# A two-layer gated attention and mixture-of-experts kernel: loads and constants enter the written order, layer 2 reuses layer 1's row tables, 256 words between scatters

## The chip, the cores and the metric

The kernel runs on one core of a Trainium2 chip. A core has TensorE (PE, with its weight loads shown apart as PEld), VectorE (DVE), ScalarE (ACT), GpSimd (POOL) and SyncE (SP), each working through its own instructions strictly in the order in which the program lists them. DMA transfers are issued by SP, by ACT and, for the indirect ones, by POOL. The metric is device time in microseconds of one execution; the figure for the kernel before is the median of three runs.

## The reference, cut to what matters

There are 4 sequences of 512 tokens with 128 channels, a context of 77 tokens for each, and two layers. Each layer adds a gated cross-attention (16 heads of 8 channels) and a gated mixture of 8 experts (128 to 512 to 128, the best two experts of each token):

```python
for l in range(2):
    # attention: LayerNorm is taken ahead of it; layer 1 adds position slopes and a mask
    q, k, v = norm(x) @ Wq.T, ctx @ Wk.T, ctx @ Wv.T
    x = x + tanh(g_xattn[l]) * (softmax(q k.T / sqrt(8)) v @ Wo.T + bo)
    # experts
    xf = norm(x)
    probs = softmax(xf @ w_router)
    w, i = top_k(probs, 2)
    x = x + tanh(g_ffn[l]) * sum_k w[k] * (gelu(xf @ w1[i[k]] + b1) @ w2[i[k]] + b2)
```

(The bias `bo` belongs to layer 0 alone.)

## The kernel before

Everything is float32 apart from the layer-1 masks. Four sequences ("batches", n = 0 to 3) go through attention one after another; batches 0 and 1 form routing group 0, batches 2 and 3 group 1. A group's 2048 token-expert pairs are sorted by expert with indirect DMAs: each token row of 130 words (128 channels, the gate weight, and the place its result goes to) is scattered twice into a table in DRAM, `xg`, in which each expert owns a region of 2048 rows. Then 16 blocks per group, 7 of 256 rows and 9 of 128, each load the weights of one expert and a piece of its rows, compute, and scatter their result rows into another table, `yk`, from which each batch loads them again in token order and adds them to x. Rows of `xg` that no token reaches must still be harmless, so the tables are cleared with zeros from a tile `fill` at the start (`clear`, lines 741 to 753), one table per layer and group: four tables, 16 stores of 1040 KB and 4 of 130 KB in all.

Every scatter goes through `Scatters.send` (line 392): POOL first writes 512 zeros into one partition of `fill` (line 394), then issues the indirect DMA (line 395). There are 64 scatters into `xg` and 92 into `yk`, 156 in all.

The order of all work is written out by hand in the string `ORDER` (lines 832 to 875). A word names a part: layer, letter, and after the dot the batch or group. The loop under it emits the instructions of each word on whatever engines it needs, so the string fixes the order on all five engines at once. The words that the text uses:

- `LS` LayerNorm statistics (DVE, then `rstd` on POOL), `LT` normalise (ACT), `LU` transpose (PE, copy on ACT), `Q` queries (PE, ACT)
- `S0` to `S3` scores of 128 tokens (PE) and their maxima (four reductions on DVE); `M`, `W0`, `W1` put the maxima into the queries; `X0` to `X3` scores again, and exp on ACT; `U0` to `U3` sums over the context; `E`, `T`, `N`, `F` the rest of attention
- `RS`, `RT`, `RU`, `RL`, `RC`, `RD`, `RM`, `RN`, `RX` the routing of one batch, up to the row numbers; `Z0` to `Z3` its scatters into `xg`, two for each word
- `RB` the group's table of blocks (DVE), `RG` its transfer into SP's registers (a PE transpose, a DVE copy, then SP reads 16 registers)
- `w`, `x`, `t`, `u`, `d`, `y` with a block number: weight load, row load (both on SP, both needing the registers), transpose, first and second matrix (PE, with GELU on ACT, bias and gate on DVE), scatter into `yk`
- `CL`, `CA` load and add the results of a batch
- `vclear`, `fill`, `clear`, `mask`, `keys`, `values`, `gate`, `routing`, `second` are words without a dot: constants and shared operands

Outside this order stand, before it, all loads of inputs (lines 68 to 98), the constants of the head slots (lines 116 to 144), the ones under the eight exp tiles `eT` (lines 146 to 150) and the zeros of the two `m_pad` tiles (lines 151 to 155). All are emitted ahead of the first word.

Of the kernel before, what the change touches and what calls it, by code (L numbers as in the profile page):

```python
# [8 lines left out]
F32 = mybir.dt.float32  # L9
# [29 lines left out]
SPARE = NFULL * 256 + NTAIL * P  # L39


@with_exitstack
def flamingo_kernel(ctx: ExitStack, tc: tile.TileContext, a: dict, out: bass.AP):
# [24 lines left out]
    x_sb = [wpool.tile([P, NT, D], F32, tag=f"x{b}", name=f"x{b}") for b in range(B)]  # L68

    def load_x(b):  # L70
        nc.sync.dma_start(out=x_sb[b], in_=a["x"][b].rearrange("(p t) d -> p t d", p=P))

    load_x(0)
    ctxT = load("ctxT", [P, B * KV], a["ctxT"], eng=nc.scalar)
    W = [{}, {}]
    for l in range(2):
        W[l]["wk"] = load(f"wk{l}", [P, 2, D], a[f"wk{l}"], eng=nc.scalar)
        W[l]["wq"] = load(f"wq{l}", [P, 2, D], a[f"wq{l}"], eng=nc.scalar)
        if l == 0:
            wv = load("wv", [P, 2 * D], a["wv"], eng=nc.scalar)  # L80
            gates = wpool.tile([P, 4], F32, tag="gates", name="gates")
            nc.scalar.dma_start(out=gates[:, 0:2], in_=a["g_xattn"].partition_broadcast(P))
            nc.scalar.dma_start(out=gates[:, 2:4], in_=a["g_ffn"].partition_broadcast(P))
        W[l]["wo"] = load(f"wo{l}", [D, D], a[f"wo{l}"])
        W[l]["router"] = load(f"router{l}", [D, E], a[f"router{l}"])
        if l == 0:
            load_x(1)
            bo = wpool.tile([P, D], F32, tag="bo", name="bo")
            nc.sync.dma_start(out=bo, in_=a["bo"].partition_broadcast(P))
    load_x(2)  # L90
    load_x(3)
    qpos_i = load("qpos_i", [P, B * NT], a["qpos"], dtype=I32)
    kpos_i = wpool.tile([P, B * KV], I32, tag="kpos_i", name="kpos_i")
    nc.sync.dma_start(out=kpos_i, in_=a["kpos"].partition_broadcast(P))
    msk_i, mskT_i = [], []
    for b in range(B):
        msk_i.append(load(f"msk{b}", [P, NT, KV], a["mask"][b].rearrange("(p t) k -> p t k", p=P), dtype=I32))
        mskT_i.append(load(f"mskT{b}", [KV, S], a["maskT"][b], dtype=I32))
# [3 lines left out]
    make_identity(nc, ident)  # L102
    mhalf = const.tile([P, NT], F32, tag="mhalf", name="mhalf")
# [12 lines left out]
    prow = counted("prow", [P, 1], [[0, 1]], channel_multiplier=1, dtype=I32)  # L116
    slot_i = const.tile([P, 2], I32, tag="slot_i", name="slot_i")
    nc.vector.tensor_scalar(slot_i[:, 0:1], prow, 15, None, ALU.bitwise_and)
    nc.vector.tensor_scalar(slot_i[:, 1:2], prow, 4, 1, ALU.arith_shift_right, ALU.bitwise_and)
    slot = const.tile([P, 2], F32, tag="slot", name="slot")  # L120
    nc.vector.tensor_copy(slot, slot_i)
    row_r = const.tile([P, 1], F32, tag="row_r", name="row_r")
    row_p = const.tile([P, 1], F32, tag="row_p", name="row_p")
    nc.vector.tensor_scalar(row_r, slot[:, 0:1], float(HD), None, ALU.is_equal)
    nc.vector.tensor_scalar(row_p, slot[:, 0:1], float(HD + 1), None, ALU.is_equal)
    base_slope = const.tile([P, 1], F32, tag="base_slope", name="base_slope")
    for g in range(HB):
        nc.vector.memset(base_slope[32 * g : 32 * g + 32, :], SLOPES[4 * g])
    k_scale, k_ones, k_slope = [], [], []
    for w in range(2):  # L130
        own = const.tile([P, 1], F32, tag=f"own{w}", name=f"own{w}")
        nc.vector.tensor_scalar(own, slot[:, 1:2], float(w), None, ALU.is_equal)
        t = const.tile([P, 1], F32, tag=f"k_scale{w}", name=f"k_scale{w}")
        nc.vector.tensor_scalar(t, own, INV_SQRT_HD, None, ALU.mult)
        k_scale.append(t)
        t = const.tile([P, 1], F32, tag=f"k_ones{w}", name=f"k_ones{w}")
        nc.vector.tensor_tensor(t, own, row_r, ALU.mult)
        k_ones.append(t)
        t = const.tile([P, 2], F32, tag=f"k_slope{w}", name=f"k_slope{w}")
        nc.vector.tensor_tensor(own, own, row_p, ALU.mult)  # L140
        nc.vector.tensor_tensor(own, own, base_slope, ALU.mult)
        for h in range(2):
            nc.vector.tensor_scalar(t[:, h : h + 1], own, SLOPES[2 * h + w] / SLOPES[0], None, ALU.mult)
        k_slope.append(t)

    eTs = []
    for i in range(8):
        t = const.tile([P, S], F32, tag=f"eT{i}", name=f"eT{i}")
        nc.vector.memset(t[64:, :], 1.0)
        eTs.append(t)  # L150
    m_pads = []
    for i in range(2):
        t = const.tile([P, NT, 2, P], F32, tag=f"m_pad{i}", name=f"m_pad{i}")
        nc.vector.memset(t, 0.0)
        m_pads.append(t)
# [230 lines left out]
    class Scatters:  # L386
# [5 lines left out]
        def send(self, to, rows, index):  # L392

            nc.gpsimd.memset(fill[:1, 0, :S], 0.0)  # L394
            i = nc.gpsimd.indirect_dma_start(  # L395
                out=to[:, :], out_offset=bass.IndirectOffsetOnAxis(ap=index, axis=0), in_=rows, in_offset=None
            )
            for other in self.sent:
                tc.declare_no_dep(i.ins, other.ins, reason="each pair has a row of its own")
            self.sent.append(i)  # L400


    class Routing:
# [13 lines left out]
        def turn(self):  # L417
# [4 lines left out]
            nc.gpsimd.tensor_copy(self.rows[:, :, :, D + 1], pair_at[:, self.b % 2])  # L422
# [92 lines left out]
        def scatter(self, b, t):  # L515
            rows, to = self.left[b]
            for k in range(2):
                self.scatters.send(xgs[self.l][self.group], rows[:, k, t, :], to[:, k, t : t + 1])
# [58 lines left out]
    class Blocks:  # L577
# [24 lines left out]
        def load_x(self, i):  # L602
            if i >= NBLK:
# [5 lines left out]
                in_=xgs[self.l][self.group][bass.ds(self.r.begins[i], n * P), :].rearrange("(s p) d -> p s d", p=P),  # L609
# [34 lines left out]
        def down(self, i):  # L644
# [23 lines left out]
            nc.vector.tensor_tensor(to[:, :n], x[:, :n, D + 1], spare[:, self.at(i) // P : self.at(i) // P + n], ALU.max)  # L668
# [7 lines left out]
    class Combine:  # L676
# [5 lines left out]
        def load(self):  # L682
            b = self.b
            self.y = act.tile([P, 2, NT, D], F32, tag="y", name="y")
            for k in range(2):
                at = SPARE + k * CAP + b % 2 * S
# [21 lines left out]
    def routing_constants():  # L708
# [4 lines left out]
        for e in range(E):  # L713
# [14 lines left out]
        pair_at = counted(  # L728
            "pair_at", [P, 2, 2, NT], [[S, 2], [CAP, 2], [1, NT]], base=SPARE, channel_multiplier=NT
        )  # L730
        spare = counted("spare", [P, SPARE // P], [[P, SPARE // P]], channel_multiplier=1)
# [3 lines left out]
    fill = const.tile([P, 2, CAP // P * PAY], F32, tag="fill", name="fill")  # L735
    xgs, yks = [], []
    for l in range(2):
        xgs.append([dram.tile([E * REGION, PAY], F32, tag=f"xg{l}{g}", name=f"xg{l}{g}") for g in range(2)])
        yks.append([dram.tile([SPARE + 2 * CAP, D], F32, tag=f"yk{l}{g}", name=f"yk{l}{g}") for g in range(2)])

    def clear(l, g):
        xg = xgs[l][g]
        for e in range(0, E, 2):
# [4 lines left out]
                in_=fill,  # L748
            )
        nc.sync.dma_start(  # L750
            out=xg[UNUSED : UNUSED + 256, :].rearrange("(p r) d -> p (r d)", p=P),
            in_=fill.rearrange("p r f -> p (r f)")[:, : 2 * PAY],
        )
# [39 lines left out]
    msk, mskT = [], []  # L793

    def mask(b):
# [5 lines left out]
        msk.append(m)  # L801
        mskT.append(mT)
# [8 lines left out]
    def part(l, name, n):  # L811
# [21 lines left out]
        vclear3 vclear0 fill vclear2 0LS.0 keys0 gate values0 0LT.0 0LS.2 0LU.0 0LS.1 0LS.3 0Q.0 0LT.1 0LT.2 values3  # L833
        0S1.0 0S0.0 0S2.0 0LU.1 0LU.2 0S3.0 0Q.1 clear10 0M.0 vclear1 mask0 0W0.0 0LT.3 0S0.1 0W1.0 0S3.1 clear00
        0X0.0 0S1.1 0Q.2 values1 mask1 0S2.2 mask2 0X1.0 0S2.1 0U0.0 0M.1 0X2.0 routing 0U1.0 0X3.0 0E0.0 0W0.1 0U2.0
        0X0.1 0T0.0 0U3.0 0X1.1 0W1.1 0U0.1 0E1.0 0S1.2 0U1.1 0T1.0 clear01 mask3 0S0.2 0E0.1 0LU.3 clear11 0N.0 0T0.1
        0X2.1 0F.0 0RS.0 0X3.1 values2 0U2.1 0RT.0 0S3.2 0U3.1 0M.2 0E1.1 second 0Q.3 0W0.2 0RU.0 0T1.1 0W1.2 0S2.3
        0N.1 0RL.0 0RC.0 0F.1 0RS.1 0X0.2 0X1.2 0RD.0 0U0.2 0X2.2 0RM.0 0RN.0 0RX.0 0U1.2 0Z0.0 0RT.1 0S1.3 0U2.2
        0RU.1 0Z1.0 0S3.3 0RL.1 0S0.3 0X3.2 0RC.1 0M.3 0RD.1 0Z2.0 0U3.2 0W0.3 0RM.1 0E0.2 0T0.2 0X0.3 0RN.1 0RX.1
        0RB.1 0E1.2 0Z3.0 0X1.3 0Z0.1 0T1.2 0N.2 0RG.1 0U0.3 0W1.3 0w0.0 0Z1.1 0F.2 0Z2.1 0Z3.1 0x0.0 0U1.3 0RS.2  # L840
        0E0.3 0X2.3 0x1.0 0X3.3 0RT.2 0w1.0 0U2.3 0U3.3 0E1.3 0T0.3 0RU.2 0T1.3 0RL.2 0N.3 0RC.2 0t0.0 0x2.0 0t1.0
        0F.3 0RD.2 0x3.0 0w2.0 0x4.0 0u0.0 0u1.0 0RS.3 0RM.2 0d0.0 0x5.0 0w3.0 0w4.0 0w5.0 0y0.0 0RT.3 0d1.0 0t2.0
        0t3.0 0RN.2 0x6.0 0u2.0 0RU.3 0RX.2 0t4.0 0w6.0 0u3.0 0x7.0 0Z0.2 0d2.0 0u4.0 0t5.0 0RL.3 0t6.0 0d3.0 0x8.0
# [109 lines left out]
```

## Time and profile before

| what | value |
|---|---|
| median of three runs | 453.98 us (452.78 to 454.99) |
| the profiled execution | 449.32 us, its span 447.6 us |
| PE busy | 394.7 us (88%) |
| POOL busy | 296.0 us (66%) |
| DVE busy | 243.9 us (54%) |
| ACT busy | 225.0 us (50%) |
| mean granted TensorE clock | 0.969 |
| moved by DMA | 81.19 MB |

The span runs from the first to the last instruction; the execution's own time lies 1.7 us above it. A busy share is an average over stages with different limits. Matmuls are pipelined and their ends are modelled, so PE counted as busy need not be at full pace. In "out<-in" the names are the program's; "idle before" is the time in which an engine sat before a group's instructions, with what ended most of it.

### The profile page before, as it was taken

What the parts mean: (1) busy time and instruction counts of PE and PEld (TensorE: products, weight loads), DVE (VectorE), ACT (ScalarE), POOL (GpSimd) and SP (SyncE); (2) the same over time, 40 slices, a digit from 0 to 9 for tenths busy, and PEclk for the clock granted to TensorE, in tenths of its full rate; (3) what the DMA queues carried; (4) which work ended last, traced back from release to release, by engine and by line L of the source; (5) the groups of instructions that cost most, each with busy time, mean ns of one, the idle gap of its engine ahead of it and who ended that gap; (6) DMA issues with size and microseconds to landing.
All of it is one profiled execution on the core that took longest, in us unless ns stands there. A gap on an engine that the chain in (4) does not pass through costs nothing.

```text
span 447.6 us, 9040 instructions
## 1 busy us (share of the span) xinstructions
PE 394.7 (88%) x2936; PEld 279.9 (63%) x2936; DVE 243.9 (54%) x929; ACT 225.0 (50%) x529; POOL 296.0 (66%) x480
## 2 busy tenths in 40 slices
PE   2399999979999599999999999999889989998960
PEld 1166345534988489996774355544378878987960
DVE  7777478763746443437682367776256533332442
ACT  3256756646564345356437764544538434433540
POOL 3478312787298889867885430698159988888870
PEclk9999999999999989999999999999689999999995
DMA  7999940014756497976613000011914568777855
GB/s 196 331 401 400 401 161 2 24 43 113 265 182 198 132 296 241 305 274 191 207 42 113 7 1 2 17 39 42 308 55 148 163 208 300 263 250 230 304 205 193
DMA packets 38526, 81.19 MB, mean 181 GB/s; under 512 B 6236, under 2 KB 20316, under 8 KB 38480
## 3 DMA queue, kind: packets, MB, share of 16 engines
q1 hardware_dynamic: 32336, 69.51, 46.6%
q0 software_dynamic: 4992, 10.30, 6.5%
q10 hardware_dynamic: 1152, 0.82, 0.7%
q8 instruction: 23, 0.38, 0.3%
q14 instruction: 23, 0.19, 0.1%
HBM read 51.69 MB, written 28.91 MB: 180 GB/s over the span
## 4 chain that ended last, share of the span: by engine, by line
PE 31%; POOL 7%; DVE 5%; DMA 4%; issue 4%; ACT 1%; SPq 0%; POOLq 0%; DVEq 0%; ACTq 0%
PE mm L649 8%; PE mm L634 7%; POOL xg L395 3%; PE mm L329 3%; DMA xb<-xg 2%; POOL fill L394 2%; PE o L343 2%; PE mm L289 2%; PE mm L326 2%; PE mm L279 1%; PE mm L266 1%; POOL yk L395 1%; PE mm L382 1%; DMA y<-yk 1%; PE mm L619 1%
## 5 line engine op out<-in xcount | busy, mean ns | idle before, releaser
L640 ACT ACTIVATE h<-mm,w 128x128 f32<-128x128 f32 (+1 forms) x256 | 86.7, 414 | 105.4 <-issue 82.6
L395 POOL DMA_INDIRECT yk<-yb,to x92 | 89.6, 974 | 20.6 <-issue 12.7
L634 PE MATMUL mm<-xbT,w 128*128 128x128 f32 (+1 forms) x512 | 92.4, 325 | 8.5 <-DVE xbT L621 6.9
L649 PE MATMUL mm<-w,h 128*128 128x128 f32 x736 | 96.6, 283 | 0.8 <-ACT h L640 0.2
L649 PEld LDWEIGHTS mm<-w,h 128*128 128x128 f32 x736 | 90.7, 194 | 5.2 <-ACT h L640 2.9
L634 PEld LDWEIGHTS mm<-xbT,w 128*128 128x128 f32 x512 | 76.2, 193 | 17.1 <-DVE xbT L621 9.1
L335 ACT ACTIVATE eT<-mm 77x512 f32<-77x512 f32 x128 | 65.3, 592 | 32.7 <-PE mm L329 32.6
L394 POOL MEMSET fill<- 1x512 f32 x156 | 80.3, 515 | 0.1
L395 POOL DMA_INDIRECT xg<-rows,rows_to x64 | 62.5, 976 | 24.2 <-issue 21.3
L657 DVE TENSOR_TENSOR yb<-mm,w 128x256 f32<-128x256 f32 (+1 forms) x64 | 22.3, 349 | 73.8 <-PE mm L649 70.9
L297 DVE TENSOR_REDUCE mx<-mm 128x4 f32<-128x308 f32 x128 | 52.1, 471 | 15.7 <-PE mm L289 15.6
L209 POOL TENSOR_SCALAR rstd<-mv 128x4 f32<-128x4 f32 x16 | 3.7, 230 | 75.1 <-DVE mv L207 35.0
L329 PE MATMUL mm<-qa,kb 32*77 32x512 f32 x256 | 43.6, 632 | 0.3 <-DVE qa L317 0.3
L343 PE MATMUL o<-eT,vb 128*32 128x512 f32 x256 | 37.5, 635 | 0.0
L621 DVE COPY xbT<-mm 128x256 f32<-128x256 f32 (+1 forms) x64 | 21.1, 344 | 25.3 <-PE mm L619 25.1
L289 PE MATMUL mm<-kb,q 32*128 32x154 f32 x512 | 30.8, 320 | 0.1
L289 PEld LDWEIGHTS mm<-kb,q 32*128 32x128 f32 x512 | 22.4, 183 | 11.7 <-issue 8.2
L663 DVE TENSOR_TENSOR yb<-yb,xb 128x256 f32<-128x256 f32 (+1 forms) x64 | 23.3, 364 | 2.2
L619 PE MATMUL mm<-ident,xb 128*128 128x128 f32 x92 | 20.0, 285 | 3.6 <-DMA xb<-xg 3.6
L329 PEld LDWEIGHTS mm<-qa,kb 32*77 32x77 f32 x256 | 11.5, 143 | 18.1 <-issue 8.7
L317 DVE TENSOR_TENSOR qa<-mm,q 128x512 f32<-128x512 f32 x16 | 11.0, 687 | 17.3 <-PE mm L315 8.9
L220 ACT ACTIVATE xn<-x,nmr,rstd 128x128 f32<-128x128 f32 x32 | 13.0, 483 | 13.2 <-DVE nmr L215 13.2
(156 smaller groups left out, 475.5 us busy)
## 6 DMA issues: line engine op xcount, KB each, us to landing
w<-in_experts SPq DMA_DIRECT2D x64, 578.0 KB, 5.1
xg<-fill SPq DMA_DIRECT2D x16, 1040.0 KB, 16.2
y<-yk SPq DMA_DIRECT2D x16, 256.0 KB, 3.2
xb<-xg SPq DMA_DIRECT2D x28, 130.0 KB, 3.8
xb<-xg SPq DMA_DIRECT2D x36, 65.0 KB, 3.9
yk<-yb,to POOLq DMA_INDIRECT x92
x<-in_x SPq DMA_DIRECT2D x4, 256.0 KB, 3.5
xg<-rows,rows_to POOLq DMA_INDIRECT x64
```

The source lines that it names most:

```text
L289: nc.tensor.matmul(view[g][:, h], lhsT=self.q[h][rows, t * P : (t + 1) * P], rhs=kbs[l][rows, h, :, b, :], start=(l == 0), stop=(l == 0 or ...
L297: nc.vector.tensor_reduce(self.mx[:, t, :, 2 * g : 2 * g + 2], view[g], AX.X, ALU.max)
L329: nc.tensor.matmul(ps[g][:KV, :], lhsT=kbs[l][rows, h, w, b, :], rhs=self.qa[h][rows, :], start=(l == 0), stop=True,)
L335: nc.scalar.activation(self.eT[j][g][:KV, :], ps[g][:KV, :], AF.Exp)
L343: nc.tensor.matmul(self.o[a][g * 32 : (g + 1) * 32, :], lhsT=vbs[self.b][:, self.l, g, j, :], rhs=self.eT[j][g], start=(w == 0), stop=(w = ...
L394: nc.gpsimd.memset(fill[:1, 0, :S], 0.0)
L395: i = nc.gpsimd.indirect_dma_start(out=to[:, :], out_offset=bass.IndirectOffsetOnAxis(ap=index, axis=0), in_=rows, in_offset=None)
L619: nc.tensor.transpose(ps[:, s * P : (s + 1) * P], x[:, s, :D], ident)
L634: nc.tensor.matmul(ps[:, g * 256 : g * 256 + n], lhsT=w[:, c * P : (c + 1) * P], rhs=xT[:, :n], start=True, stop=True,)
L640: nc.scalar.activation(h[:, c, :n], ps[:, g * 256 : g * 256 + n], AF.Gelu_apprx_tanh, bias=w[:, B1_AT + c : B1_AT + c + 1])
L649: nc.tensor.matmul(y[:, s * P : (s + 1) * P], lhsT=h[:, c, s * P : (s + 1) * P], rhs=w[:, W2_AT + c * P : W2_AT + (c + 1) * P], start=(c = ...
L663: nc.vector.tensor_tensor(yb[:, :n, :], yb[:, :n, :], x[:, :n, D : D + 1].to_broadcast([P, n, D]), ALU.mult)
```

## The change

Six things, in one diff.

1. The input loads become functions (`load_x`, `load_q`, `load_o`, `load_gates`, `load_positions`, `load_mask`), and so do the slot constants (`slots`), the ones under `eT` (`ones_below`, four tiles at a time) and the zeros of `m_pad`. New words call them: `ldx0`, `ldq0`, `ldo0`, `ldgates`, `ldpos`, `ldmask0`, `ldctx`, `ldwv`, `slots`, `ones0`, `pads0` and so on. The second layer's query and key weights are issued by SP in place of ACT.
2. There is one `xg` table per group, shared by both layers, in place of one per layer and group. It is cleared once, in two halves (`cleara`, `clearb`), 8 stores of 1040 KB in all. The second layer scatters over the first one's rows; to tell old rows from new, its result places start at `ROWS` in a `yk` table of twice the height, and its `spare` places too, so that an old row's place loses against the spare one in the maximum of line 668.
3. `fill` has half the size, and a store reads it twice.
4. The spacer before each scatter writes 256 words of a tile of its own, `apart`, in place of 512 words of `fill`.
5. `pair_at` and `spare` exist once per layer.
6. `ORDER` is written anew throughout.

```diff
+ROWS = SPARE + 2 * CAP
...
-    load_x(0)
-    ctxT = load("ctxT", [P, B * KV], a["ctxT"], eng=nc.scalar)
...
+    def load_q(l):
+        for n in ("wk", "wq"):
+            W[l][n] = load(f"{n}{l}", [P, 2, D], a[f"{n}{l}"], eng=nc.scalar if l == 0 else nc.sync)
...
+    def load_gates():
+        gates = wpool.tile([P, 4], F32, tag="gates", name="gates")
+        nc.scalar.dma_start(out=gates[:, 0:2], in_=a["g_xattn"].partition_broadcast(P))
+        nc.scalar.dma_start(out=gates[:, 2:4], in_=a["g_ffn"].partition_broadcast(P))
+        bo = wpool.tile([P, D], F32, tag="bo", name="bo")
+        nc.sync.dma_start(out=bo, in_=a["bo"].partition_broadcast(P))
+        return gates, bo
...
+    def load_mask(b):
+        msk_i[b] = load(f"msk{b}", [P, NT, KV], a["mask"][b].rearrange("(p t) k -> p t k", p=P), dtype=I32)
+        mskT_i[b] = load(f"mskT{b}", [KV, S], a["maskT"][b], dtype=I32)
...
+    apart = const.tile([1, S // 2], F32, tag="apart", name="apart")
...
+    def ones_below(i):
+        for t in eTs[4 * i : 4 * i + 4]:
+            nc.vector.memset(t[64:, :], 1.0)
...
-            nc.gpsimd.memset(fill[:1, 0, :S], 0.0)
+            nc.gpsimd.memset(apart, 0.0)
...
-            nc.gpsimd.tensor_copy(self.rows[:, :, :, D + 1], pair_at[:, self.b % 2])
+            nc.gpsimd.tensor_copy(self.rows[:, :, :, D + 1], pair_at[self.l][:, self.b % 2])
...
-                self.scatters.send(xgs[self.l][self.group], rows[:, k, t, :], to[:, k, t : t + 1])
+                self.scatters.send(xgs[self.group], rows[:, k, t, :], to[:, k, t : t + 1])
...
-            nc.vector.tensor_tensor(to[:, :n], x[:, :n, D + 1], spare[:, self.at(i) // P : self.at(i) // P + n], ALU.max)
+            nc.vector.tensor_tensor(to[:, :n], x[:, :n, D + 1], spare[self.l][:, self.at(i) // P : self.at(i) // P + n], ALU.max)
...
-                at = SPARE + k * CAP + b % 2 * S
+                at = ROWS * self.l + SPARE + k * CAP + b % 2 * S
...
-    fill = const.tile([P, 2, CAP // P * PAY], F32, tag="fill", name="fill")
+    fill = const.tile([P, CAP // P * PAY], F32, tag="fill", name="fill")
+    xgs = [dram.tile([E * REGION, PAY], F32, tag=f"xg{g}", name=f"xg{g}") for g in range(2)]
...
+        yks.append([dram.tile([ROWS * (l + 1), D], F32, tag=f"yk{l}{g}", name=f"yk{l}{g}") for g in range(2)])
+
+    def clear(g, q):
+        xg = xgs[g]
+        for e in range(4 * q, 4 * q + 4, 2):
...
+                in_=fill.unsqueeze(1).to_broadcast([P, 2, CAP // P * PAY]),
...
     ORDER = """
-        vclear3 vclear0 fill vclear2 0LS.0 keys0 gate values0 0LT.0 0LS.2 0LU.0 0LS.1 0LS.3 0Q.0 0LT.1 0LT.2 values3
-        0S1.0 0S0.0 0S2.0 0LU.1 0LU.2 0S3.0 0Q.1 clear10 0M.0 vclear1 mask0 0W0.0 0LT.3 0S0.1 0W1.0 0S3.1 clear00
...
-        0N.1 0RL.0 0RC.0 0F.1 0RS.1 0X0.2 0X1.2 0RD.0 0U0.2 0X2.2 0RM.0 0RN.0 0RX.0 0U1.2 0Z0.0 0RT.1 0S1.3 0U2.2
-        0RU.1 0Z1.0 0S3.3 0RL.1 0S0.3 0X3.2 0RC.1 0M.3 0RD.1 0Z2.0 0U3.2 0W0.3 0RM.1 0E0.2 0T0.2 0X0.3 0RN.1 0RX.1
-        0RB.1 0E1.2 0Z3.0 0X1.3 0Z0.1 0T1.2 0N.2 0RG.1 0U0.3 0W1.3 0w0.0 0Z1.1 0F.2 0Z2.1 0Z3.1 0x0.0 0U1.3 0RS.2
...
-        0w9.0 0x9.0 0y2.0 0d7.0 0w10.0 0Z3.2 0t8.0 0Z0.3 0RG.3 0t9.0 0w0.1 0x10.0 0w11.0 0u8.0 0Z1.3 0d8.0 0x11.0
...
+        ldmask2 ldx0 ldpos ones0 ldgates slots ldq0 0LS.0 pads0 ldwv ldx2 ldctx gate vclear1 vclear2 0LT.0 ldx1 keys0
+        0LU.0 ldmask0 0LS.2 values1 0Q.0 0LS.1 ones1 0LT.2 0LT.1 values2 0S0.0 0S2.0 0S1.0 ldx3 0LU.1 vclear0 0LU.2
+        0S3.0 0Q.1 0M.0 values0 ldo0 0W0.0 0S1.1 0S3.1 0X0.0 fill 0W1.0 0Q.2 routing 0LS.3 pads1 ldmask3 0X1.0 0U0.0
...
+        ldmask1 0S1.3 mask1 0F.1 0X0.2 0X1.2 0RD.0 0RS.1 0U0.2 0X2.2 0RM.0 0RN.0 0RX.0 0U1.2 clearb0 0Z0.0 0RT.1 0S3.3
+        ldo1 0E0.2 0M.3 0U2.2 0RU.1 0X3.2 0W0.3 0RL.1 0RC.1 0T0.2 0X0.3 0RD.1 0U3.2 0RM.1 0E1.2 0X1.3 0Z1.0 0U0.3
+        0T1.2 0W1.3 0RN.1 0RX.1 0RB.1 0N.2 0X2.3 0U1.3 0F.2 0Z2.0 0E0.3 0X3.3 0U2.3 0Z3.0 0Z0.1 0Z1.1 0RS.2 clearb1
+        0U3.3 0RG.1 0E1.3 0Z2.1 0Z3.1 0RT.2 0T0.3 0T1.3 0N.3 0w0.0 0w1.0 0x0.0 0x1.0 0RU.2 0F.3 0x2.0 0RL.2 0x3.0
+        0RS.3 0RC.2 0RD.2 0RT.3 0x4.0 0w2.0 0RM.2 0RN.2 0RU.3 0RX.2 0w3.0 0t0.0 0t1.0 0Z0.2 0u0.0 0t2.0 0u1.0 0Z1.2
...
+        0d10.0 0x15.0 0w14.0 0t12.0 0t13.0 0y7.0 0y8.0 0w15.0 0RG.3 0d11.0 0u12.0 0t14.0 0x0.1 0w0.1 0u13.0 0d12.0
+        0x1.1 0t15.0 0u14.0 0w1.1 0y9.0 0d13.0 0u15.0 0t0.1 0d14.0 0u0.1 0w2.1 0t1.1 0x2.1 0d15.0 0x3.1 0y10.0 0u1.1
...
```

## The prediction

> **What bounds it now.** I read the shares by engine first, then the stretches, then the chain of waits, then the timeline at the places these named. The stretches (columns: from:to, length, busy time of PE, PE weight loads, DVE, ACT and POOL with counts, granted clock, DMA share, GB/s) show where PE, the fullest engine, loses time:
>
> ```profile
> 0.00:24.00 24.00, 8.96 (x16) 4.05 (x16) 17.36 (x74) 6.67 (x13) 10.70 (x44) 1.00 0.86 273
> 24.00:36.00 12.00, 11.88 (x120) 8.36 (x120) 10.29 (x29) 7.58 (x17) 7.43 (x15) 1.00 1.03 402
> 144.00:156.00 12.00, 6.77 (x50) 5.64 (x48) 6.05 (x32) 3.42 (x12) 10.72 (x15) 1.00 0.46 129
> 313.00:337.00 24.00, 20.18 (x108) 13.18 (x101) 9.61 (x44) 11.09 (x24) 9.07 (x14) 0.79 0.51 169
> 341.00:436.00 95.00, 86.10 (x628) 79.05 (x627) 40.13 (x165) 42.43 (x123) 82.68 (x114) 1.00 0.72 235
> ```
>
> The reader is to see an empty front, a hole at 144 to 156, a slow piece at a clock of 0.79, and 95 us in which POOL has work without a break: its 82.68 us hold 57 spacer and scatter pairs, and each pair has a further 0.17 us of issue gap. The groups on POOL and the chain give that cadence:
>
> ```profile
> L395 POOL DMA_INDIRECT yk<-yb,to x92 | 89.6, 974 | 20.6 <-issue 12.7 <-DVE to L668 5.6 <-DVE nmr L215 0.7
> L394 POOL MEMSET fill<- 1x512 f32 x156 | 80.3, 515 | 0.1
> L180 POOL MEMSET vb<- 128x1024 f32 x4 | 3.8, 950 | 0.0
> ```
>
> ```profile
> 307.44 0.96 POOL xg L395
> 308.41 0.51 POOL fill L394
> 308.92 0.17 issue
> 309.09 0.96 POOL xg L395
> 310.05 0.51 POOL fill L394
> 310.56 0.17 issue
> 310.73 2.27 DMA xg<-rows,rows_to
> ```
>
> One scatter every 0.96 + 0.51 + 0.17 = 1.645 us; the last lands 2.27 us after its issue, and only then does the first block's row load leave. The timeline shows the front and the hole:
>
> ```profile
> 5.13 4.27 DVE L149 MEMSET eT<- 64x512 f32 x8
> ...
> 12.03 1.79 DVE L886 MEMSET fill<- 128x2080 f32 x1 [0.38 <-issue]
> ...
> 13.74 0.23 DVE L206 BATCH_NORM_STATS2 st<-x 128x6 f32<-128x128 f32 x1
> ...
> 19.91 3.78 PE L266 MATMUL mm<-xnT,wq 128*128 128x512 f32 x4 [0.67 <-ACT xnT L230]
> ...
> 150.62 0.27 PE L569 MATMUL mm<-ident,begin 128*1 128x128 f32 x1 [1.80 <-DVE begin L564]
> ...
> 157.21 0.48 PE L619 MATMUL mm<-ident,xb 128*128 128x128 f32 x1 [2.42 <-DMA xb<-xg]
> ```
>
> DVE clears tiles until 13.7 before the first statistics; and at 150.6 the table of group 1 (0RG.3) stands in PE's and SP's order between blocks of group 0, so SP, waiting for that register, sends the next row load only at 153.29, which lands at 157.2.
>
> To compare the two orders I add up PE work ahead of a word, each part at the price at which the chain has it when nothing holds it (S 0.74, X 1.03, U 1.00, Q 1.72, layer 1's mask additions 0.55 and 0.86, and per 128 rows t 0.22, u 0.87, d 0.90). All parts make 360 us: the span's 447.6 holds some 87 us of loss, about 20 of it before 24 us and 15 after the last matmul.
>
> **The change part by part.**
>
> *Spacer.* From 0.202 us (128x128 memsets) and 0.950 (128x1024): 0.835 ns a word on 0.095 us, which gives 0.522 for 512 words (measured 0.515) and 0.309 for 256. So 0.206 us less per scatter, a cadence of 1.44; bounds 0 (the scatter takes the time back) and 0.26 (half the spacer). I take 0.206, as scatter rows are 0.963 to 0.964 at minimum and median, with no sign of back-pressure. Over 156 scatters POOL loses 32 us, worth something only where POOL paces.
>
> [...] Were scatters served one at a time the spacer would save nothing and the first rival's sum would hold; but a cadence of 1.645 is already under 2.27, so they overlap.
>
> *Front.* Ahead of 0LS.0 stand on DVE now only half the eT clears (4 x 0.485, say until 2.7) and the slot constants (1.55 to 4.98 before, 3.4), so statistics begin near 6.4 in place of 13.74. x0 is SP's third issue, 0.9 us later; with 3.5 us to landing and 308 KB of mask ahead at 388 GB/s (0.8 us; the rate about 3 us in, from the DMA digits of the first 30 us) it lands near 6.0: hidden, and 1 to 2 us would show if DVE were free sooner. From statistics to Q.0 took 6.2 us; keys0's four ACT copies (2.1), formerly in the idle front, now stand between norm and transpose copy, of which 1.6 shows: Q.0 near 14.2, 5.7 us earlier. The first queries, weights and context leave ACT after the gates, the context as sixth at about 3.0, in for keys0's matmuls at 7. Moved behind the first scores on DVE: 0LS.3 (1.8), one m_pad (0.91), half the fill (0.90) = 3.6 us, into a stretch with DVE at 10.29 of 12; half shows. -4 (-5.7 to -2).
>
> [...]
>
> *Layer 0, first scatters to first block.* Z0.0 to the row load took 81.1 to 109.15, 16 scatters, with 0RT.1's copies between. 16 x 0.206 = -3.3. 0S1.3 and 0S0.3 move ahead of Z0.0 (1.5 us more PE work), but 2.0 us more is done by 0t0.0. New wait: 0RS.2's rstd stands on POOL before Z2.1, and the four scatters behind it wait for 0F.2, whose result came 22 us after Z0.0; POOL needs 18 us to get there. 0 to 3 us; with fewer scores between, I take 0.8. -3 (-5 to +1).
>
> *The hole.* 0RG.3 goes from PE position 107.9 to 115.2, behind all of group 0's loads, and 0Z0.2 from 89.6 to 77.7. That closes a hole of 5.2 us (144 to 156). Late next is group 1: 0RG.3 to 0t0.1 has 6.6 us of PE work, and the register, issue and landing took 150.6 to 157.2, also 6.6. -3 (-6 to 0).
>
> *Layer 1, first scatters.* -3.3 again; 1Z0.0 stands 3.6 us of PE work later, with 2.1 more done by 1t0.0. -1 net, rounded against the gain (-3.4 to +2; -3.3 + 3.6 - 2.1 is -1.8).
>
> *Layer 1, blocks.* 1Z0.2 moves from 268.0 to 278.5, 10.5 later, with 5.4 us of POOL work drawn ahead of it: +5.1 on a POOL-paced end. The 60 scatters from there save 60 x 0.206 = 12.4. POOL alone gives -7.3; PE, which took 112.6 us for 98.3 from 321 on, can give back at most 14. Where POOL stops pacing, the h and yb handovers remain. -5 (-12 to +1).
>
> *Nothing:* the clears (16 to 8 large stores) lie at 14 to 50 us, before the first scatter at 81, on a queue whose next load is at 109; were they late, Z0.0 would wait for clearb0, up to 20 us to landing. Masks are converted on POOL where it was idle (48 to 60: 0.34 us busy) and are read in layer 1 only. Two more iotas are 0.35 us there. ldq1 on SP comes long before keys1. Layer 1's scatters into shared rows must follow layer 0's reads, the last issued at 212.6; the first scatter is at 285. The tail (1CL, 1CA behind 1y15.1) is the same; one spacer, 0.2.
>
> Sum: -4 - 3 - 3 - 1 - 5 = -16 on the profiled 449.3 (span 447.6 and 1.7 around it): 433. That execution lies 4.7 below the median 454.0; the same distance makes it **438**.
>
> **Rivals.**
> 1. *The scatter takes back what the spacer gives* (slower). Place: POOL's pairs of line 394 and 395. At 1.645 the terms are front -4, layer 0 +0.3, hole -1 (order alone), layer 1 +2.3 and +5.1: +2.7, 457. Break-even is 0.206 x 2.7 / 18.7 = 0.03 us saved, a cadence of 1.61; at 1.70 the 133 scatters in paced places (16, then 41 from 126 to 194, 16, 60) add 7, which makes 463. I write 459, between. For it: landing takes 2.27, so overlap grows. Against: constant 0.963. 0.17.
> 2. *POOL is no longer what paces the blocks, and the gain stops there.* For it: 384 to 396 has PE at 12.00 of 12 with POOL at 10.82. Against: no POOL idle from 341 to 412. Hole and blocks 0: -8, 446. 0.22.
> 3. *DVE eats it.* DVE has 10.29 of 12 at 24 to 36 and 10.40 at 84 to 96; if the moved 3.6 shows whole (+1.8) the four held scatters wait 3 us and not 0.8 (+2.2), and the hand-over to group 1 costs the same 3, rival 2's -8 becomes -1: 453. 0.08.
> That the shared rows make layer 1 wait has 70 us of slack against it and gets no chance of its own.
>
> **Numbers.** The forecast has 0.53. Its own range is 427 to 446: all terms at their best would make -32, so I stop at -27, and at the upper end it meets rival 2. The range is 427 to 457, with some 0.12 above (the worse half of rival 1) and 0.05 below. Half a per cent, 2.3 us, is what a measurement of this kernel can tell from no change. Faster: forecast and rival 2, 0.53 + 0.22 = 0.75; same: rival 3, 0.08; slower: rival 1, 0.17.
>
> **What would show it.** Spacer rows near 0.31, scatter rows still 0.96; Q.0's first matmul near 14; no PE hole after 0RG.3; first row load of layer 0 some 6 us earlier; POOL with idle time in layer 1's last 90 us. Wrong if scatter rows pass 1.1, if POOL waits on rstd inside the first 16 scatters for over 3 us, or if 1Z0.2 starts later than 329 and POOL is full to the end.

## The result, and the profile after

The changed kernel took 481.38 us in the median of four runs (476.06 to 486.85), the kernel before 453.38 us beside it: a ratio of 1.054, 95% interval [1.044, 1.063], clearly slower. (The ratio leaves out two of the four runs, the profiled one among them, as disturbed; the other two took 476.06 and 479.45 us.) The profiled execution took 486.85 us with a span of 485.0.

What the prediction looked for first is there. In the groups of the changed kernel (count, then busy time and mean ns of one, then the idle time ahead of it) spacer and scatter have the durations that were foreseen:

```profile
L399 POOL DMA_INDIRECT yk<-yb,to x92 | 89.8, 977 | 81.4 <-DVE to L672 42.0 <-DVE xbT L625 24.3 <-issue 11.0
L399 POOL DMA_INDIRECT xg<-rows,rows_to x64 | 62.7, 980 | 19.2 <-issue 9.8 <-DVE rows_to L516 6.1 <-DVE over L536 2.7
L398 POOL MEMSET apart<- 1x256 f32 x156 | 47.0, 301 | 0.1
```

The spacer went from 515 to 301 ns, the scatter stayed at 0.98 us, and the cadence is 0.96 + 0.30 + 0.17 = 1.43 us. But GpSimd now idles 81.4 us ahead of the block scatters (20.6 before), waiting for VectorE. The stretches (PE, PE weight loads, VectorE, ScalarE and GpSimd busy, clock, DMA share, GB/s) show where:

```profile
0.00:24.00 24.00, 13.37 (x63) 7.21 (x64) 16.89 (x76) 10.03 (x21) 10.69 (x35) 1.00 0.39 119
...
137.00:161.00 24.00, 13.88 (x91) 12.48 (x90) 7.18 (x33) 5.25 (x13) 20.20 (x32) 0.85 0.54 165
...
372.00:400.00 28.00, 15.66 (x105) 14.27 (x104) 7.45 (x34) 5.94 (x18) 24.60 (x39) 0.87 0.56 173
```

The front is fuller (13.37 of 24 in place of 8.96). In the blocks, though, at 137 to 161 and at 372 to 400, PE is busy little more than half of the time, VectorE and ScalarE less than a third, while GpSimd sends scatter after scatter (16 in a row from 137.3 to 158.8, 22 from 368.1 to 398.8). Three timelines of one such place, PE first ("remote" and "issue" stand where the profile finds nobody who ended the wait):

```profile
144.04 2.05 PE L653 MATMUL mm<-w,h 128*128 128x128 f32 x16
145.93 1.89 PE L638 MATMUL mm<-xbT,w 128*128 128x256 f32 x8
147.66 0.27 PE L623 MATMUL mm<-ident,xb 128*128 128x128 f32 x1
148.78 1.16 PE L638 MATMUL mm<-xbT,w 128*128 128x128 f32 x8 [0.84 <-DVE xbT L625]
156.90 1.23 PE L653 MATMUL mm<-w,h 128*128 128x128 f32 x4 [6.96 <-issue]
```

```profile
156.37 0.84 ACT L644 ACTIVATE h<-mm,w 128x256 f32<-128x256 f32 x2 [11.71 <-issue]
```

```profile
153.44 0.42 DVE L661 TENSOR_TENSOR yb<-mm,w 128x256 f32<-128x256 f32 x1 [4.72 <-remote]
...
159.95 0.29 DVE L625 COPY xbT<-mm 128x128 f32<-128x128 f32 x1 [5.56 <-remote]
```

Each of the three readers needs nothing but a result that PE has on record long before. The block's addition of line 661 reads the sixteen matmuls recorded as over at 146.1 and starts at 153.4; the Gelu reads the first four of the eight from 145.93 and starts at 156.4; the copy of line 625 reads the transpose of 147.66 and starts at 159.95, 12 us late. The semaphore steps in the trace agree: PE's step for that transpose is at 159.93. I call such a result *late*, by the time from a matmul's recorded end to PE's semaphore step for it. In the trace before no result is late by more than 0.12 us up to 300 us; after, about 30 results in the first 200 us are late by more than 1 us, the worst by 12.1. The stretches with such delays begin inside runs of scatters, mostly two to seven scatters in, and end about where the run does.

### The profile page after: what moved, and what is told of

Its sections match the earlier page's. It is cut to its first block, busy times and chain, and to the rows that moved or that the text cites. A ratio compares the mean times of both kernels' runs of the same rounds, so it can differ in the third digit from the quotient of the medians.

```text
span 485.0 us, 9037 instructions
## 1 busy us (share of the span) xinstructions
PE 403.5 (83%) x2936; PEld 289.2 (60%) x2936; DVE 242.8 (50%) x929; ACT 226.7 (47%) x529; POOL 263.2 (54%) x482
## 4 chain that ended last, share of the span: by engine, by line
PE 65%; issue 10%; DMA 7%; DVE 7%; POOL 5%; ACT 3%; another core or an unknown queue 1%; SPq 1%; ACTq 0%; POOLq 0%; DVEq 0%
PE mm L653 13%; PE mm L638 12%; PE mm L333 8%; PE o L347 7%; PE mm L293 6%; POOL yk L399 3%; PE mm L270 3%; PE mm L330 3%; DMA y<-yk 2%; PE mm L386 2%; PE mm L623 2%; PE mm L283 2%; DMA xb<-xg 2%; PE mm L232 2%; DVE mx L301 1%
## 5 line engine op out<-in xcount | busy, mean ns | idle before, releaser
L399 POOL DMA_INDIRECT yk<-yb,to x92 | 89.8, 977 | 81.4 <-DVE to L672 42.0
L653 PE MATMUL mm<-w,h 128*128 128x128 f32 x736 | 99.9, 290 | 24.7 <-ACT h L644 11.0
L653 PEld LDWEIGHTS mm<-w,h 128*128 128x128 f32 x736 | 94.5, 205 | 28.9 <-ACT h L644 12.7
L638 PE MATMUL mm<-xbT,w 128*128 128x128 f32 (+1 forms) x512 | 98.6, 339 | 14.6 <-DVE xbT L625 6.8
L638 PEld LDWEIGHTS mm<-xbT,w 128*128 128x128 f32 x512 | 80.1, 201 | 23.8 <-DVE xbT L625 8.2
L398 POOL MEMSET apart<- 1x256 f32 x156 | 47.0, 301 | 0.1
L625 DVE COPY xbT<-mm 128x128 f32<-128x128 f32 (+1 forms) x64 | 21.6, 344 | 46.0 <-PE mm L623 15.0
L333 PE MATMUL mm<-qa,kb 32*77 32x512 f32 x256 | 40.6, 622 | 0.0
L293 PE MATMUL mm<-kb,q 32*128 32x154 f32 x512 | 32.2, 333 | 0.3 <-DVE mx L301 0.3
L293 PEld LDWEIGHTS mm<-kb,q 32*128 32x128 f32 x512 | 23.6, 195 | 14.4 <-issue 7.5
L623 PE MATMUL mm<-ident,xb 128*128 128x128 f32 x92 | 21.7, 299 | 1.6 <-DMA xb<-xg 1.1
L210 DVE BATCH_NORM_STATS2 st<-x 128x6 f32<-128x128 f32 x64 | 17.1, 268 | 10.4 <-POOL x L698 9.4
L330 PE MATMUL mm<-mbT,ident 77*77 77x512 bf16 x64 | 18.5, 381 | 1.8 <-ACT eT L339 0.5
```

The source lines that it names most:

```text
L293: nc.tensor.matmul(view[g][:, h], lhsT=self.q[h][rows, t * P : (t + 1) * P], rhs=kbs[l][rows, h, :, b, :], start=(l == 0), stop=(l == 0 or ...
L330: nc.tensor.matmul(ps[g][:KV, :], lhsT=ident16[:KV, :KV], rhs=mskT[b], start=True, stop=False)
L333: nc.tensor.matmul(ps[g][:KV, :], lhsT=kbs[l][rows, h, w, b, :], rhs=self.qa[h][rows, :], start=(l == 0), stop=True,)
L398: nc.gpsimd.memset(apart, 0.0)
L399: i = nc.gpsimd.indirect_dma_start(out=to[:, :], out_offset=bass.IndirectOffsetOnAxis(ap=index, axis=0), in_=rows, in_offset=None)
L623: nc.tensor.transpose(ps[:, s * P : (s + 1) * P], x[:, s, :D], ident)
```

## The experiments

Eighteen runs in six groups; the runs of a group share a chip and a set of runs of the kernel before. They fall into two kinds, told apart by the traces:

| group | chip | before | 256 words, new order | other kernels | PE late, first 200 us |
|---|---|---|---|---|---|
| on record | ? | 453.4 | 481.4 | | up to 12.1 us |
| 1 | 8 | 451.0 | | `new_512` 441.0, `old_256` 450.5, `new_384` 427.3 | 0.1 |
| 2 | 5 | 453.3 | `after_again` 425.1 | `new_256_wide` 425.0, `new_320` 426.1, `new_256_breath` 424.9 | 0.1 |
| 3 | 10 | 453.9 | `after_third` 469.9 | `new_then_old` 478.5, `new_unshared` 471.9 | 5.0 to 6.0 |
| 4 | 7 | 455.6 | | `old_256_b` 488.3, `new_512_b` 441.2 | 7.7 and 0.6 |
| 5 | 10 | 452.0 | | `new_384_b` 428.9, `new_448` 433.7, `new_256_breath_b` 425.8 | 0.1 |
| 6 | 5 | 451.9 | | `new_then_old_b` 480.5, `new_384_c` 432.1, `new_256_breath_c` 450.5 | 7.7, 0.8, 6.4 |

**The width of the spacer, alone and undone.** At first the short cadence stood accused, against the new order and against the shared tables.

```diff
-    apart = const.tile([1, S // 2], F32, tag="apart", name="apart")
+    apart = const.tile([1, S], F32, tag="apart", name="apart")
```

> The changed kernel with its spacer back at 512 words (about 0.51 us, cadence about 1.65 us); order, loads and shared tables stay changed. In the changed kernel TensorE's matmuls are recorded on time in stretches of scatters without a gap (117 to 134, 137 to 160, 213 to 230, 372 to 396 us), but what reads their result starts up to 12 us later (the transpose recorded at 147.66 is copied at 159.95). Theory A (scatters that follow each other at 1.43 us hold TensorE up): these delays go, the time is 440 to 457 us, at or under that before. Theory B (the new order and its in-order waits cost the time): nothing of it goes and GpSimd gets 156 x 0.21 = 33 us more work, 480 to 495 us. Theory C (the shared tables or the loads moved to SP's queue cost it): as B, 478 to 495 us.

```diff
-            nc.gpsimd.memset(fill[:1, 0, :S], 0.0)
+            nc.gpsimd.memset(fill[:1, 0, : S // 2], 0.0)
```

> The kernel before with nothing changed but the spacer: 256 words in place of 512, cadence about 1.43 us. Theory A: slower than before, 460 to 480 us, with results of TensorE read microseconds after their matmuls were recorded, in the stretches of scatters without a gap (81 to 95 us and in both layers' blocks). Theories B and C: the old order gets the shorter cadence for nothing, 440 to 453 us, with no such delays.

```diff
-    apart = const.tile([1, S // 2], F32, tag="apart", name="apart")
+    apart = const.tile([1, 3 * S // 4], F32, tag="apart", name="apart")
```

> The changed kernel with a spacer of 384 words (about 0.41 us, cadence about 1.54 us). Theory A: between the changed kernel and the one with 512 words; 445 to 472 us, nearer the upper end if the delay grows with the number of scatters in a row, at the lower end if there is a cadence from which the scatters are absorbed. Theories B and C: 478 to 490 us.

Measured against the kernel before: 512 words in the new order 0.986 [0.978, 0.993], 256 in the old order 1.004 [0.999, 1.008], 384 in the new order 0.954 [0.947, 0.961]. None has a late result in the part that can be matched. Theory B and C fell with the first and third run: the new order with its loads and shared tables is no loss. But A fell too, as it stood: the old order at 1.43 us, with runs of 22 and 24 scatters, had no delay. And its gain was nothing, for a reason that its groups show:

```profile
L395 POOL DMA_INDIRECT yk<-yb,to x92 | 89.9, 977 | 41.6 <-DVE to L668 25.7 <-issue 11.5 <-DVE xbT L621 2.4
L395 POOL DMA_INDIRECT xg<-rows,rows_to x64 | 62.5, 976 | 31.0 <-issue 22.6 <-DVE xbT L621 3.3 <-DVE nmr L215 2.0
L394 POOL MEMSET fill<- 1x256 f32 x156 | 47.0, 301 | 0.1
```

Ahead of its scatters GpSimd idled 41.6 + 31.0 = 72.6 us, 44.8 before (20.6 + 24.2): 27.8 of the 33 us that the shorter spacers saved went into waiting, most of it for VectorE's `to` (25.7, 5.6 before).

**The changed kernel again, and where its tiles lie.** A narrower `apart` may also move the tiles behind it, so that was a theory of its own.

> The changed kernel itself, once more. With 384 words it took 427 us and with 512 words 441 us, and in neither do TensorE's results come late; the kernel before with 256 words (runs of 22 and 24 scatters at 1.43 us) has no such delay either. Theory A2 (256 words in the new order hold TensorE up): 474 to 488 us again, with the delays. Theory R (what was measured was of one chip or one session and doesn't come back): 420 to 440 us, no delays.

```diff
-    apart = const.tile([1, S // 2], F32, tag="apart", name="apart")
+    apart = const.tile([1, S], F32, tag="apart", name="apart")
...
-            nc.gpsimd.memset(apart, 0.0)
+            nc.gpsimd.memset(apart[:, : S // 2], 0.0)
```

> The changed kernel with the place of the 512-word spacer and the work of the 256-word one: apart is 512 words wide, and 256 of them are cleared. Every tile behind it lies where it lies in the run with 512 words. Theory L (the narrow spacer moved all later tiles in SBUF, and TensorE's reads suffer from where they lie): 420 to 440 us, no delays. Theory A2 (the cadence of 1.43 us itself): 472 to 488 us with delays. Theory R: 420 to 440 us.

(`new_320` has `5 * S // 8` words.)

> The changed kernel with 320 words (about 0.355 us, cadence about 1.49 us). Theory A2 with a sharp edge between 1.43 and 1.54 us: either about 425 to 432 us (edge below 1.49) or 440 to 480 us with delays (edge above). Theory R: 422 to 430 us, as 256 and 384 would be.

```diff
-            nc.gpsimd.memset(apart, 0.0)
+            for _ in range(3 if len(self.sent) % 8 == 7 else 1):
+                nc.gpsimd.memset(apart, 0.0)
```

> The changed kernel with its 256-word spacer, but three of them instead of one ahead of each eighth scatter: the mean cadence is about 1.53 us, as with 384 words, and in between seven scatters follow at 1.43 us. Theory A2 as a backlog (scatters come faster than their DMA ends, and the queue behind them fills): the pause drains it, 425 to 440 us, no delays. A2 as a matter of each pair's distance: delays stay, 465 to 485 us. Theory L: delays stay, 470 to 488 us. Theory R: 422 to 435 us.

The unchanged program took 425.06 us, 0.937 [0.927, 0.947] of the kernel before, with no late result. The other three are level with it: 425.0, 426.1 and 424.9. So where results are on time it is of no account where the tiles lie (that their place does not make the delay either shows only later, in `old_256_b`, which moves no tile and is late), and what was put on record did not come back here. The same place of the program, PE and then VectorE, in that run:

```profile
137.09 1.95 PE L653 MATMUL mm<-w,h 128*128 128x128 f32 x16
138.88 1.89 PE L638 MATMUL mm<-xbT,w 128*128 128x256 f32 x8
140.61 0.27 PE L623 MATMUL mm<-ident,xb 128*128 128x128 f32 x1
```

```profile
139.08 0.42 DVE L661 TENSOR_TENSOR yb<-mm,w 128x256 f32<-128x256 f32 x1 [0.41 <-PE mm L653]
...
140.92 0.29 DVE L625 COPY xbT<-mm 128x128 f32<-128x128 f32 x1 [0.89 <-PE mm L623]
```

PE's records have nearly the same spacing (1.79 and 1.73 us from start to start, 1.89 and 1.73 on record), and both readers now start within 0.05 us of PE's end, in the midst of scatters at the same 1.43 us. The stretch around it and layer 1's blocks:

```profile
132.00:156.00 24.00, 23.40 (x190) 22.30 (x189) 11.91 (x53) 11.04 (x37) 21.13 (x34) 1.00 0.87 288
...
330.00:410.00 80.00, 73.37 (x547) 68.83 (x545) 30.75 (x126) 34.46 (x107) 64.09 (x103) 0.96 0.78 254
```

**A third time, with two parts of the change undone.**

> The changed kernel a third time, on whichever chip it gets: 474 to 488 us were measured first, 421 to 426 us the second time. Theory S (how long TensorE's results take is a matter of the chip that runs it, and the changed kernel meets it there): either value, with late results of TensorE in the trace if and only if it is the slow one. Theory R (the first measurement was a single event): 420 to 430 us, no late results.

`new_then_old` has the new order up to `0y15.1` and the old order for all that is left; only ORDER differs.

> The changed kernel with the new order up to the last block of layer 0 and the order before from there on (with 256 words, shared tables and the moved loads). In the second run of the changed kernel layer 0's first group of blocks (first up to the second group's first up) took 47.0 us in place of 61.1, and layer 1 from its first row load to its last matmul 108.2 in place of 120.2. Theory O (the order itself made both gains): layer 0 keeps its 14 us and layer 1 gives back its 12, 434 to 441 us. Theory K (in layer 1 it is the shorter cadence and not the order): 423 to 430 us.

```diff
-    xgs = [dram.tile([E * REGION, PAY], F32, tag=f"xg{g}", name=f"xg{g}") for g in range(2)]
+    xgs = [[dram.tile([E * REGION, PAY], F32, tag=f"xg{l}{g}", name=f"xg{l}{g}") for g in range(2)] for l in range(2)]
...
-... cleara1 mask0 ...
+... cleara1 clearc0 cleard0 mask0 ...
...
-... clearb1
+... clearb1 clearc1 cleard1
```

> The changed kernel with a table of its own for each layer, layer 1's cleared beside layer 0's (10 more transfers, 8.8 MB more, issued by SP behind those of layer 0). As the prediction had it, the clears hide and cost nothing: 420 to 428 us. If the transfers hold up the expert weights that SP issues behind them or their traffic collides with the first row loads: 428 to 436 us.

The delays came back in all three: 469.9 (1.028 [1.018, 1.039]), 478.5 (1.056 [1.048, 1.065]) and 471.9 (1.038 [1.027, 1.050]). Theory R fell, S seemed to hold. Within the group the old order for layer 1 takes some 9 us longer than the new one in the medians (477 to 486 us against 463 to 475); with separate tables the time can't be told from the changed kernel's (467 to 476).

**Is it the order or the cadence that meets the delay?** The same two kernels as at first, to meet such a group:

> The kernel before with 256 words, again, to meet the chip on which the changed kernel is slow (the chips of the runs so far: two on which TensorE's results are on time, 421 to 429 us for the changed kernel, and one on which they come late, 463 to 475 us). On the late chip every late stretch begins with the third to seventh scatter of an unbroken run at 1.43 us and ends with the run. Theory A3 (on that chip scatters 1.43 us apart hold TensorE up, in any order of the work): 465 to 485 us there, late results; 447 to 453 us on the other chips, as before. Theory B3 (on that chip it takes the new order too): 445 to 455 us on all.

> The changed kernel with 512 words, again, for the same reason. Theory A3: 438 to 445 us on every chip, no late results, since 1.64 us leaves TensorE its time. Theory B3: 465 to 485 us with late results on the late chip, 438 to 445 us on the others.

These two runs settle it. In this group the old order with 256 words took 488.3 us, 1.074 [1.056, 1.091], with results up to 7.7 us late; the new order with 512 words took 441.2 us, 0.970 [0.953, 0.987]. Theory A3 holds, B3 falls: here the cadence alone costs some 33 us in the old order (488.3 against 455.6). The new order with 256 words did not run in this group; against its 441.2 us with 512 words stand 469.9 and 481.4 us in the other late groups. The stretches of the old order with 256 words, first where results were on time (group 1), then here:

```profile
148.00:160.00 12.00, 8.64 (x52) 7.49 (x52) 3.86 (x20) 3.54 (x12) 10.65 (x18) 0.86 0.73 221
160.00:172.00 12.00, 11.25 (x77) 10.32 (x78) 4.93 (x18) 7.48 (x20) 10.48 (x18) 1.00 0.90 280
172.00:184.00 12.00, 12.00 (x99) 11.64 (x98) 6.01 (x22) 5.08 (x16) 5.35 (x9) 1.00 0.81 243
```

```profile
148.00:160.00 12.00, 6.28 (x45) 5.40 (x45) 5.37 (x31) 3.53 (x12) 9.70 (x15) 0.99 0.40 110
160.00:172.00 12.00, 7.97 (x47) 7.08 (x47) 4.17 (x13) 3.69 (x10) 10.50 (x18) 0.87 0.84 277
172.00:184.00 12.00, 9.61 (x33) 7.90 (x34) 2.17 (x9) 3.84 (x12) 7.58 (x12) 0.57 0.46 143
```

The same program at the same time of its run gets 228 matmuls done in these 36 us, and 125 where results are late.

**Where the edge lies.** 384 words and pauses had been tried only where results were on time.

> The changed kernel with 384 words (cadence about 1.54 us), to see where on a late chip the edge lies: there 256 words (1.43 us) took 463 to 488 us in both orders, 512 words (1.64 us) 440 to 443 us. Edge theory (each scatter holds TensorE up for a fixed time, and the delay grows only where the next comes before it is made good): 1.54 us is either clear of it, 426 to 432 us as on the other chips with no late results, or still in it, with 440 to 465 us. On an on-time chip: 425 to 429 us.

(`new_448` has `7 * S // 8` words.)

> The changed kernel with 448 words (about 0.46 us, cadence about 1.59 us). Edge theory: 430 to 438 us on a late chip, with no late results; on an on-time chip the same. If the late chips are only slower by degrees: 440 to 450 us there.

> The changed kernel with 256 words and three of them ahead of each eighth scatter. On an on-time chip 423 to 429 us. On a late chip: if a queue fills behind the scatters and a pause empties it, 425 to 440 us; if each pair's distance counts, it stays at 455 to 475 us, with late results that end at the pauses.

This group got the chip number of the third group and yet had no late result: 428.9, 433.7 and 425.8 us. So theory S fell as well; it is not a matter of the chip. The question was put once more:

> The new order up to layer 0's last block and the order before behind it, again: its first run fell where TensorE's results come late (with 256 words between scatters), which covered the answer. The same chip number has since given 426 to 430 us with 384 words and with pauses, so lateness belongs to the session and not to the chip. Where results are on time: theory O (the order made both layers' gains) 434 to 441 us; theory K (layer 1's gain is the cadence's) 423 to 430 us. Where they are late: 470 to 486 us again.

> 384 words once more, for a late session. Where results are on time: 426 to 430 us. Where they are late: 426 to 434 us if 1.54 us between scatters is clear of the edge, 440 to 465 us if not.

> 256 words with two more ahead of each eighth scatter, for a late session. On time: 423 to 429 us. Late: 425 to 440 us if pauses empty a queue, 455 to 475 us if each pair's distance counts.

This time results were late, on the chip number of the second group. The spliced order took 480.5 us again, 384 words 432.1 us (0.957 [0.950, 0.964]), and 256 words with pauses 450.5 us (0.996 [0.993, 1.000]). With 1.54 us between all scatters the worst delay in the first 200 us is 0.8 us (2.7 up to 400 us); with about the same mean made of seven short steps and a pause it is 6.4. In layer 1 the late stretches end about at the pauses, and 450.5 us lies between the two forecasts, so neither holds as it stood: pauses let a part of the delay run off, even steps avoid most of it. Most of the loss comes between 1.54 and 1.43 us. One answer is missing: the spliced order was never met where results are on time, so the share of the on-time gain that layer 1's order has was not measured. The stretch from 137 to 161 in three late groups, for 256 (`after_third`), 384 (`new_384_c`) and 512 words (`new_512_b`), in this order:

```profile
137.00:161.00 24.00, 18.92 (x129) 17.12 (x127) 8.31 (x36) 6.69 (x19) 21.13 (x34) 0.93 0.64 190
```

```profile
137.00:161.00 24.00, 21.65 (x177) 20.30 (x176) 9.44 (x42) 10.78 (x36) 21.29 (x32) 1.00 0.92 297
```

```profile
137.00:161.00 24.00, 22.72 (x189) 21.71 (x187) 10.74 (x51) 11.85 (x40) 21.47 (x30) 1.00 0.84 271
```

The new order with 384 words beats the kernel before and the changed one on record, in every group it ran in: 427.3, 428.9 and 432.1 us, 0.946 to 0.957.

## Why the prediction was wrong, point by point

The spans, cut at four events of the traces, hold most of the answer (us; in brackets the difference to before):

| stage | before | on record | `after_again` | `new_384` | `new_512` | `old_256` |
|---|---|---|---|---|---|---|
| start to layer 0's first scatter | 81.1 | 81.0 | 80.8 (-0.3) | 81.1 (0) | 80.4 (-0.7) | 81.5 (+0.4) |
| to layer 0's first block matmul | 34.5 | 36.8 (+2.3) | 33.0 (-1.5) | 33.5 (-1.0) | 34.8 (+0.3) | 32.2 (-2.3) |
| to layer 1's first scatter | 169.5 | 188.9 (+19.4) | 161.8 (-7.7) | 163.3 (-6.2) | 167.5 (-2.0) | 169.5 (0) |
| to layer 1's first row load | 28.0 | 29.4 (+1.4) | 25.5 (-2.5) | 25.6 (-2.4) | 29.5 (+1.5) | 27.0 (-1.0) |
| to the end | 134.5 | 148.9 (+14.4) | 122.3 (-12.2) | 121.9 (-12.6) | 125.6 (-8.9) | 135.8 (+1.3) |

**The step that failed is the spacer's bound.** It took the saved 0.206 us in full since the scatter rows were constant, "with no sign of back-pressure", and its lower bound was 0. The rows stayed constant, at 973 to 985 ns in the mean, in late groups and others alike. The price was not paid on GpSimd's rows, where the first rival and "wrong if scatter rows pass 1.1" looked for it, but in PE's results, and it went below the bound: at 256 words 45 to 56 us are lost where results are late (470 and 481 against 425), on record +19.4 and +14.4 us in the two stages with block scatters. The first rival had the sign, and closer scatters as what sets it off, but neither the place nor the size (its 457 to 463 us). One of the prediction's signs, GpSimd with idle time in layer 1, did come, but on record it came because GpSimd waited behind the late results. No row of the trace before shows such a delay, so the size could not be read there; the bound of 0, however, was more than the constant row gave.

**Where results are on time, the sign holds, and the sizes and their split between order and cadence don't.** 425 us is 2 us below the range's lower end; the sum of -16 was -24.

- *Front, -4.* It was -0.3. The landing of x0, put at 6.0 us, 0.8 of it for the mask ahead of it, and called hidden, kept VectorE waiting for 0.81 us, until 6.88; Q.0's first matmul went from 19.91 to 15.23 us, and the first scatter stayed where it was (trace on record):

```profile
6.88 0.29 DVE L210 BATCH_NORM_STATS2 st<-x 128x6 f32<-128x128 f32 x1 [0.81 <-DMA x<-in_x]
```

```profile
15.23 3.78 PE L270 MATMUL mm<-xnT,wq 128*128 128x512 f32 x4 [1.12 <-ACT xnT L234]
```

```profile
80.95 1.25 POOL L399 DMA_INDIRECT xg<-rows,rows_to  x1 [0.69 <-DVE nmr L219]
```

  In `after_again` PE is busy for 3.8 us more up to 84 us (72.6 against 68.8, by 12 us stretches), of which the clock of 0.86 from 24 to 36 us, 1.00 before, takes by estimate 12 x 0.14 = 1.7. The rest is work that the new order has put ahead of the scatter, among it 0S1.3 and 0S0.3, which the prediction had counted only against the next term.
- *Layer 0, first scatters to first block, -3.* It was -1.5. The row load leaves at 109.62 in `after_again` (109.15 before), and it is not what comes last. The chain of that run:

```profile
110.38 0.12 DVE rows L480
110.51 0.07 DVE nmr L219
110.58 0.10 DVE m L486
110.68 0.03 DVE before L489
110.72 0.11 issue
110.83 0.60 PE mm L501 x2
111.43 0.57 PE mm L502 x2
112.00 0.91 PE mm L232 x4
112.91 0.44 PE mm L623 x2
```

  Batch 2's routing (0RN.2, line 501) and batch 3's transposes (0RU.3, line 232) stand on PE ahead of the first block's transposes (line 623). PE sits idle for 5.01 us ahead of line 501, waiting for VectorE's choice of batch 2, a wait that the new order added and the prediction missed.
- *The hole and group 1, -3; layer 1's first scatters, -1; layer 1's blocks, -5.* They were -7.7, -2.5 and -12.2, the last at its lower bound. The prediction priced the order at -1, +2.3 and +5.1 and the cadence at the rest, and added them. But with 512 words the new order gives -2.0, +1.5 and -8.9 by itself, the cadence alone in the old order 0, -1.0 and +1.3, and both together more than their sum: 10 us for the order (451.0 to 441.0), nothing for the cadence (451.0 to 450.5), 28 for the two (453.3 to 425.1). In the old order the saved time went into waiting (the 27.8 us above), so the shorter cadence is worth something here only where scatters stand so that their data are there. The prediction's own sum for the new order at 1.645 us was +2.7; `new_512` is that kernel and measures -10. The mis-sized term is layer 1's blocks: counted in PE work ahead of 1Z0.2, the order looked 5.1 us worse there; it is 8.9 better.
- *Rival 2, GpSimd no longer paces.* Its mechanism is right below 384 words, its price of 446 us is not: 384, 320 and 256 words give 427, 426 and 425 us. With 512 words GpSimd is full to the end of layer 1, 59 scatters without a gap, and with 384 words it still is, 60 scatters from 322.1 to 413.5 us. First 512 words, then 384:

```profile
329.00:424.00 95.00, 84.04 (x615) 77.85 (x614) 39.27 (x161) 41.54 (x120) 85.36 (x116) 0.96 0.74 234
```

```profile
322.00:413.00 91.00, 83.64 (x622) 77.65 (x620) 37.82 (x160) 42.00 (x122) 80.68 (x118) 0.98 0.78 247
```

  (Each pair has a further 0.17 us of issue gap.) At 256 words it is busy for 64.09 of 80 us there (the stretch 330 to 410 above).
- *Nothing for the clears and moved loads.* Separate tables with 10 more stores cost nothing that could be told from the changed kernel, 471.9 against 469.9 us in a late group; on time this was not tried, and the moved loads were never undone by themselves.

## What to carry to other kernels

A pause that looks idle can protect another engine: shorten it by steps and stop where the time stops falling, here at 384 words, since the last step gained some 2 us where results were on time and cost 38 to 49 us where they were late (432.1 against 469.9 and 481.4, in different groups). A shorter cadence and an order are not to be priced apart and added: here the one had value only where the other had the data ready. And a surprising result is worth one more run of the very same program before it is explained: here 481, 425 and 470 us.

## What the runs showed of the hardware

In some groups, indirect scatters 1.43 us apart make TensorE's results late, by up to 12.1 us (on record), while at the place compared its matmuls are recorded at nearly the same spacing as on time (1.89 and 1.73 us on record, 1.79 and 1.73 in `after_again`). It is TensorE alone: measured in the same way in the trace on record, no step of ScalarE, VectorE or GpSimd is late by more than 0.04 us up to 460 us. Even at the first scatter, which follows no other, one result is 0.6 us late in every late group (0.63 on record), with 256, 384 and 512 words alike; where results are on time it is 0.1 or less. With 1.64 us between scatters it stays at 0.6 us (`new_512_b`), with 1.54 it grows to 2.7 by 400 us (`new_384_c`), with 1.43 to between 5.0 and 12.1 in the first 200 us (the table of groups).

What makes a group late is open. Chip numbers 5 and 10 were met both ways, and the kernel before does not tell: its medians are 451 to 456 us in all groups. The late traces share one thing more: they hold 5,100 to 6,500 semaphore records, the others 7,800 to 8,100. These losses begin with the scatters. Up to 80 us, ahead of the first one, `after_third`, `new_384_c` and `new_512_b` hold 544 records of DMA landings each, as `after_again` and `new_512` do; from 80 to 160 us they hold 476, 583 and 883, where `after_again` has 1288 and `new_512` 1190. But missing records alone are not the delay: `new_384_c` lacks as many in all (5,173 are left) as the trace on record and is only 3 to 5 us slower than its like. Whether results would be late without the recording was not tried: every execution here was recorded.
